# A scan kernel in which GpSimd adds two states before TensorE sums them, in 16 of 128 steps

## The chip, the cores and the metric

The kernel runs on one core of one Trainium2 chip. The metric is the time of one execution on the device in microseconds, given as the median of several runs. The profile is of one execution of its own; its times are counted from the start of its span.

The engines are named as in the profile: PE is TensorE (matmuls), PEld its weight loads, DVE is VectorE, ACT is ScalarE, POOL is GpSimd, SP is the engine that issues most transfers.

## The reference, cut to what matters

The program is two layers, each an attention-like part and an MLP, with layer norms and residuals around them. The first part is a selective scan over 512 time steps for 2 sequences, 1024 channels and 16 states per channel:

```python
def step(state, inp):
    dt_t, B_t, C_t, u_t = inp
    dA = jnp.exp(dt_t[..., None] * A)
    state = state * dA + (dt_t * u_t)[..., None] * B_t[:, None, :]
    y = jnp.einsum('bdn,bn->bd', state, C_t)
    return (state, y)
...
y = ys.transpose(1, 0, 2) + x * D
y = y * jax.nn.silu(gate)
return y @ W_out.T
```

Then follow an MLP whose weights are stored as 4-bit numbers and dequantised by the kernel, an attention over heads with single-head keys and values, and an MLP with a shared and a routed part. All sums are in fp32. The output y of a channel is a sum over its 16 states; in which order they are added is free up to rounding.

## The kernel before, in words

**The scan.** Channels lie on the 128 partitions, time along the free axis. A *block* is one sequence's chunk of 128 channels; there are 16 blocks, the eight of sequence 0 first (`order`, L993). Each block is worked in eight *steps* (`gi`) of two states (`NG = 2`), so that there are 128 steps `s`. A tile `bx` of 128 x 2 x 512 goes through four engines in a step:

- `times_B` (L1012, VectorE): bx = du x B, where du = dt x u lies in PSUM;
- `scan` (L1020, VectorE): the recurrence along time over the two states, with the decays `da`, which `exps` (L997, ScalarE) has written to PSUM;
- `times_C` (L1026, GpSimd): bx = bx x C;
- `sums` (L1030, TensorE): two matmuls with the identity add the two halves of bx to the block's sum `py` in PSUM. The first step of a block begins the sum with a matmul by diag(D).

`fin` (L1044, VectorE) multiplies the gate g by the finished sum, two steps into the next block. There is one bank for py: the next block's first matmul (L1036) waits for fin. There are six buffers for bx, so `times_B` of a step waits for the sums of six steps before.

**The order.** A loop over s writes the order of every engine's queue by hand; `pin` (L401) ties each instruction to the one before it on its engine. In the pass for step s, TensorE gets the sums of step s - 2 and some matmuls of other work; VectorE gets the product for s + 1 and the scan of s; GpSimd gets the product with C of s. An engine works through its queue strictly in this order.

**The other work of TensorE.** The generator `stream` (L956) hands out the matmuls that are to run beside the scan, one call at a time, in a fixed order. While sequence 1 is scanned these are: sequence 0's output projection (`out_tiles`, L904, `po`, L916), the transposes of the normed rows (`turned`, L777), and sequence 0's first MLP (`ffn0`, L938: for each of eleven tiles of the hidden layer four matmuls for `fg` and four for `fu`, L947). How many calls are handed out in a pass is set by a budget `free`: it grows by `STEP = 3.5` us a pass, each call costs `MM = 0.86`, the sums of the pass cost 0.86 for each matmul, and of what is unspent at most 0.86 is kept. A call can also be refused because neither of two PSUM banks is free, or because its input isn't due yet; then the budget of the pass is lost.

What is done with a result is a *job*, started two ticks (one pass) after its last matmul: for an MLP tile, ScalarE evicts the gate (L682 to L684), GpSimd multiplies (L687), and VectorE multiplies with `fu` (L935); for a row tile of the output projection, `out_job` (L865) copies it (L868), norms it (L119 to L134, L150), adds it to x (L855) and norms again. GpSimd jobs take turns (`pool_turn`).

**After the scan.** What is left of `stream` runs off. Then come sequence 1's output projection (L1124), the down projection of sequence 0's MLP (L1146), and the rest of the program. The down projection's weights are dequantised in this stage by `once` (L309): VectorE takes the nibbles out (L233) and subtracts the zeros (L322), GpSimd multiplies with the scales (L323), SP writes them to HBM (L330 for the first part, L340 for the second), from where SP loads them as `wd` (L1141). The tiles for it take the memory that the scan's tiles held. Weight tiles (w4: W_out, gate and up weights, `wd`) share three buffers.

Of the kernel before, what the change touches and what calls it, by code (L numbers as in the profile page):

```python
# [28 lines left out]
NCH = D_IN // P  # L29
N_ST = 16  # L30
# [4 lines left out]
NG = 2  # L35
NGI = N_ST // NG
# [20 lines left out]
def tile_sandwich(  # L57
# [5 lines left out]
    nc = tc.nc  # L63
# [24 lines left out]
    ident = const.tile([P, P], F32, name="ident")  # L88
# [312 lines left out]
    def pin():  # L401

        seen = nc.cur_bb.bb.instructions
        for ins in seen[behind.get("n", 0) :]:
            if ins.engine not in ORDERED:
                continue
            prev = behind.get(ins.engine)
            if prev is not None:
                tc.add_manual_dep(
                    ins, prev.name,  # L410
                    mybir.DependencyInfo(mybir.DependencyClass.NoSync, mybir.DependencyReason.DATA),
                    reason="order of tracing",
                )
            behind[ins.engine] = ins
        behind["n"] = len(seen)
# [6 lines left out]
    with ExitStack() as mamba:  # L422
# [35 lines left out]
        st = {}  # L458
# [21 lines left out]
        def diag(k):  # L480

            c = k % NCH
            t_ = dgp.tile([P, P], F32, tag="dg", name=f"dg{k}")
            nc.scalar.activation(t_, ident, AF.Copy, scale=ch[:, c, KCONV + 1 : KCONV + 2])
            st["diag", k] = t_
# [49 lines left out]
        def states(b, gi):  # L535

            for lst, lo, nm in ((Bbs[b], 0, "B"), (Cbs[b], R_C - R_B, "C")):
                t_ = bcp.tile([P, NG, S], F32, tag=f"{nm}{gi}", name=f"{nm}{b}_{gi}")
                n0 = lo + gi * NG
                ins = nc.sync.dma_start(  # L540
                    out=t_, in_=scr[b][n0 : n0 + NG, :].partition_broadcast(P)
                )
                lst[gi] = t_
            return ins

        def dt_in(b, c):
            ps = mbank(f"pv{b}_{c}")
            nc.tensor.matmul(ps, wdt[:, ts(c, P)], dtT[b], start=True, stop=True)
            return ps
# [9 lines left out]
        with ExitStack() as p1:  # L559
# [78 lines left out]
            for gi in range(NGI):  # L638
                last = states(0, gi)
# [10 lines left out]
        with ExitStack() as p2:  # L650
# [17 lines left out]
            def spawn(gen, lag=0):  # L668
                jobs.append([now[0] + lag, gen])

            def tick():
                now[0] += 1
                for job in list(jobs):
                    if job[0] <= now[0]:
                        try:
                            job[0] = now[0] + next(job[1])
                        except StopIteration:
                            jobs.remove(job)
# [13 lines left out]
            def bank_free():  # L692
                return len(turns) < 2 or turns[-2][1] is not None
# [10 lines left out]
            MM = 0.86  # L704
# [288 lines left out]
            order = [(b, c) for b in range(B) for c in range(NCH)]  # L993
            NS = len(order) * NGI
            bxs = {}

            def exps(s):  # L997
                k, gi = divmod(s, NGI)
                b, c = order[k]
                for i in range(NG):  # L1000
                    n = gi * NG + i
                    nc.scalar.activation(  # L1002
                        das[s % 2][:, i, 1:], st["dt", b, c][:, 1:], AF.Exp, scale=A[:, c, n : n + 1]
                    )

            def new_du(k):

                b, c = order[k]
                du = st["du"] = ps_du.tile([P, S], F32, tag="du", name=f"du{b}_{c}")
                nc.scalar.copy(du, st["dt", b, c])  # L1010

            def times_B(s):  # L1012
                k, gi = divmod(s, NGI)
                b, c = order[k]
                if gi == 0:
                    nc.vector.tensor_mul(st["du"], u[b][c], st["du"])
                bx = bxs[s] = bxp.tile([P, NG, S], F32, tag="bx", name=f"bx{b}_{c}_{gi}")
                nc.vector.tensor_mul(bx, st["du"].unsqueeze(1).to_broadcast([P, NG, S]), Bbs[b][gi])  # L1018

            def scan(s):  # L1020
                flat = bxs[s].rearrange("p n t -> p (n t)")
                nc.vector.tensor_tensor_scan(  # L1022
                    flat, das[s % 2].rearrange("p n t -> p (n t)"), flat, 0.0, ALU.mult, ALU.add
                )

            def times_C(s):  # L1026
                b, c = order[s // NGI]
                nc.gpsimd.tensor_mul(bxs[s], bxs[s], Cbs[b][s % NGI])  # L1028

            def sums(s):  # L1030
                k, gi = divmod(s, NGI)
                b, c = order[k]
                cost = NG * MM
                if gi == 0:
                    y = st["y"] = ps_y.tile([P, S], F32, tag="y", name=f"py{b}_{c}")
                    nc.tensor.matmul(y, st["diag", k], u[b][c], start=True, stop=False)  # L1036
                    cost += MM
                bx = bxs.pop(s)
                for i in range(NG):
                    n = gi * NG + i  # L1040
                    nc.tensor.matmul(st["y"], ident, bx[:, i, :], start=False, stop=(n == N_ST - 1))  # L1041
                return cost

            def fin(k):  # L1044

                b, c = order[k]
                nc.vector.tensor_mul(g[b][c], g[b][c], st["y"])
                st[f"fin{k}"] = now[0]

            def dt_job(k, ps):  # L1050
                dt_out(*order[k], ps)
                release(f"pv{k}")
                yield 1
# [9 lines left out]
            for s in range(NS + 3):  # L1063
                k, gi = divmod(s, NGI)
                free = min(free, MM) + STEP
                if gi == 1 and k + 1 < len(order):
                    dt_due = k + 1
                if gi == 2 and k:
                    fin(k - 1)
                for part in ((1, 0) if gi == 2 else (0, 1)):  # L1070
                    if part == 0:
                        if 0 <= s - 2 < NS:
                            free -= sums(s - 2)
                    else:
                        while free > 0 and s < NS:
                            if dt_due and bank_free():
                                turns.append([f"pv{dt_due}", None])
                                spawn(dt_job(dt_due, dt_in(*order[dt_due])), 2)
                                free -= MM
                                dt_due = None  # L1080
                            cost = next(pe, None)
                            if cost is None:
                                break
                            free -= cost
                tick()
                if gi == 4 and k + 1 < len(order):
                    diag(k + 1)
                if 0 < s < NS - 1:
                    times_B(s + 1)
                    if gi == NGI - 2 and k + 1 < len(order):  # L1090
                        new_du(k + 1)
                tick()
                if s < NS:
                    scan(s)
                    if s == 0:
                        times_B(1)
                    if s + 2 < NS:
                        exps(s + 2)
                    times_C(s)
                    if order[k] == (0, NCH - 1):  # L1100
                        states(1, gi)
                pin()
# [6 lines left out]
        with ExitStack() as p3:  # L1109
# [9 lines left out]
            for j in range(NCH // 2):  # L1119
                w = wo_pair(1, 0, j)  # L1120
                for e in range(2):
                    c = 2 * j + e
                    for i in range(TB):
                        nc.tensor.matmul(  # L1124
                            po[i], g[1][c][:, ts(i, P)], w[:, e, :],
                            start=(c == 0), stop=(c == NCH - 1),
# [9 lines left out]
            for i, m in enumerate(IC):  # L1136
                j, e = divmod(i, 2)
                if not e:
                    w = wst.tile([P, 2, H], F32, tag="w4", name=f"wd0_{j}")
                    n = len(IC[i : i + 2])  # L1140
# [4 lines left out]
                for t in range(TB):  # L1145
                    nc.tensor.matmul(  # L1146
                        fo[t], its[i][:m, ts(t, P)], w[:m, e],
                        start=(i == 0), stop=(i == len(IC) - 1),
# [279 lines left out]
```

## Time and profile before

| | |
|---|---|
| median of 3 runs | 965.91 us (965.67 to 966.76) |
| profiled execution | 963.47 us, span 961.7 us |
| mean granted TensorE clock | 0.971 |
| busy over the span | PE 90%, DVE 70%, POOL 48%, ACT 44% |
| first and last scan instruction | start at 74.2 and 568.9 us |
| products with C (L1028) | 128, 2360 ns each |
| scans (L1022) | 128, 2277 ns each |
| sums (L1041) | 512 matmul records, two to a matmul call of 128 x 512 fp32 |

Of a group's line in the profile, the first part tells line, engine and operation, what is written and read and its shape, and how often; behind the bar stand the total busy time in us and the mean of one in ns; behind the second bar the idle time of that engine just ahead of these instructions, with what ended most of it. In a timeline, a line has the start and the length in us, then the instructions that follow each other directly, merged. In a list of waits, a line has who waited for whom, the total in us, how many times, and the longest.

### The profile page before, as it was taken

How to read it: one execution, taken by the hardware profiler on the slowest of the kernel's cores; microseconds unless marked ns; L12 is line 12 of the kernel's file. 1: busy time of each engine (PE TensorE's matmuls, PEld its weight loads, DVE VectorE, ACT ScalarE, POOL GpSimd, SP SyncE). 2: the span in 40 equal slices, each digit the busy share in tenths (PEclk: the TensorE clock that was granted, in tenths of full speed). 3: DMA queues.
4: the chain of work that ended last, by engine and by line, in shares of the span. 5: the costliest groups of instructions: out<-in, count | busy, mean ns of one | idle time of the engine just before them, and what ended most of it. 6: DMA issues, size and time to landing. Idle time of an engine off the chain costs nothing.

```text
span 961.7 us, 7188 instructions
## 1 busy us (share of the span) xinstructions
PE 869.3 (90%) x2216; PEld 391.1 (41%) x2216; DVE 676.8 (70%) x783; ACT 420.7 (44%) x631; POOL 464.0 (48%) x335
## 2 busy tenths in 40 slices
PE   6967979878999799769999999998999998999994
PEld 3533433323543344324443434444544444445441
DVE  5959999999999989999989977334510024525225
ACT  4245775656667646565656421124320013412122
POOL 6656796776877757777767664330000000001002
PEclk9988999999999999999999999999999999999998
DMA  6349011100003833300110114336122231100101
GB/s 200 143 159 394 22 37 37 37 29 30 22 26 134 295 128 131 110 0 5 40 44 22 29 40 147 133 127 212 55 62 74 63 100 44 65 12 22 55 0 44
DMA packets 43816, 80.08 MB, mean 83 GB/s; under 512 B 7774, under 2 KB 20937, under 8 KB 43778
## 3 DMA queue, kind: packets, MB, share of 16 engines
q1 hardware_dynamic: 41506, 73.64, 22.6%
q0 software_dynamic: 1984, 5.47, 1.5%
q10 hardware_dynamic: 288, 0.52, 0.1%
q8 instruction: 17, 0.28, 0.1%
q14 instruction: 21, 0.17, 0.1%
HBM read 68.37 MB, written 11.24 MB: 83 GB/s over the span
## 4 chain that ended last, share of the span: by engine, by line
PE 49%; DVE 27%; issue 10%; POOL 5%; DMA 3%; ACT 1%; SPq 0%; DVEq 0%; POOLq 0%; ACTq 0%
DVE bx L1022 10%; PE py L1041 8%; DVE bx L1018 8%; PE pd L1356 6%; PE pup L1293 5%; PE fo L1146 4%; PE fu L367 3%; PE fo L1209 3%; PE fg L367 3%; PE fu L947 3%; POOL bx L1028 3%; PE po L1124 3%; PE fg L947 2%; DMA B<-scr 2%; DVE u L475 2%
## 5 line engine op out<-in xcount | busy, mean ns | idle before, releaser
L1028 POOL TENSOR_TENSOR bx<-bx,C 128x1024 f32<-128x1024 f32 x128 | 302.1, 2360 | 134.3 <-DVE bx L1022 118.1
L1022 DVE TENSOR_TENSOR_SCAN bx<-da,bx 128x1024 f32<-128x1024 f32 x128 | 291.4, 2277 | 0.1
L1041 PE MATMUL py<-bx,ident 128*128 128x512 f32 x512 | 249.0, 617 | 38.3 <-POOL bx L1028 38.2
L1002 ACT ACTIVATE da<-dt,A 128x511 f32<-128x511 f32 x256 | 176.6, 691 | 163.2 <-DVE bx L1022 158.5
L1041 PEld LDWEIGHTS py<-bx,ident 128*128 128x128 f32 x512 | 96.6, 195 | 171.9 <-issue 96.9
L1018 DVE TENSOR_TENSOR bx<-du,B 128x1024 f32<-128x1024 f32 x128 | 154.0, 1204 | 9.5 <-DMA wgu_d<-w_gu 6.2
L1222 DVE TENSOR_TENSOR it<-it,fu 128x512 f32<-128x512 f32 (+1 forms) x11 | 7.6, 687 | 73.9 <-PE fu L367 73.9
L1293 PE MATMUL pup<-hT_l,wup 128*128 128x512 f32 x128 | 57.2, 602 | 0.0
L709 PE MATMUL pg<-xT,w_g 128*128 128x512 f32 x120 | 56.3, 597 | 0.0
L1356 PE MATMUL pd<-wdn,hid 128*128 128x512 f32 x128 | 56.3, 601 | 0.0
L381 POOL TENSOR_TENSOR sd<-ve,half 128x4 f16<-128x4 f16 x2 | 2.1, 1044 | 110.5 <-DVE ve L379 110.5
L127 POOL TENSOR_TENSOR rs_lo<-ve_lo,mhalf 128x1 f32<-128x1 f32 x8 | 5.5, 683 | 78.3 <-DVE ve_lo L125 78.3
L947 PE MATMUL fu<-hT_f,wu 128*128 128x512 f32 (+1 forms) x88 | 41.5, 593 | 0.7 <-ACT dt L553 0.7
L947 PE MATMUL fg<-hT_f,wg 128*128 128x512 f32 (+1 forms) x88 | 41.6, 595 | 0.0
L367 PE MATMUL fg<-hT_f,wg 128*128 128x512 f32 (+1 forms) x88 | 40.2, 593 | 0.7 <-ACT hT_f L171 0.7
L367 PE MATMUL fu<-hT_f,wu 128*128 128x512 f32 (+1 forms) x88 | 40.7, 603 | 0.0
L475 DVE SCALAR_TENSOR_TENSOR u<-px,ch,u 128x511 f32<-128x511 f32 (+2 forms) x48 | 35.8, 746 | 6.1 <-ACT u L468 4.9
L1209 PE MATMUL fo<-wd,it 128*128 128x512 f32 (+1 forms) x88 | 39.8, 595 | 0.0
L1146 PE MATMUL fo<-wd,it 128*128 128x512 f32 (+1 forms) x88 | 38.0, 593 | 0.0
L1356 PEld LDWEIGHTS pd<-wdn,hid 128*128 128x128 f32 x128 | 24.9, 194 | 31.8 <-issue 31.2
L1293 PEld LDWEIGHTS pup<-hT_l,wup 128*128 128x128 f32 x128 | 24.5, 195 | 28.8 <-issue 28.8
L1221 ACT ACTIVATE it<-fg 128x512 f32<-128x512 f32 (+1 forms) x11 | 6.6, 597 | 65.7 <-PE fg L367 65.7
(223 smaller groups left out, 1137.8 us busy)
## 6 DMA issues: line engine op xcount, KB each, us to landing
wo<-in_W_outT SPq DMA_DIRECT2D x20, 512.0 KB
B<-scr SPq DMA_DIRECT2D x16, 512.0 KB
C<-scr SPq DMA_DIRECT2D x16, 512.0 KB
wg<-wgu_d SPq DMA_DIRECT2D x10, 512.0 KB
wu<-wgu_d SPq DMA_DIRECT2D x10, 512.0 KB
w_x<-in_W_in SPq DMA_DIRECT2D x8, 512.0 KB
wgu_d<-w_gu POOLq DMA_DIRECT2D x16, 256.0 KB, 2.3
w_g<-in_W_in SPq DMA_DIRECT2D x8, 512.0 KB
```

The lines of the kernel that those rows point to most:

```text
L367: nc.tensor.matmul(ps[:m], w[:, kc, e * P : e * P + m], hT[:, kc, :], start=(kc == 0), stop=(kc == KH - 1),)
L709: nc.tensor.matmul(ps, w[:, k, ts(e, P)], xT[b][:, k, :], start=(k == 0), stop=(k == KH - 1))
L947: nc.tensor.matmul(ps[:m], wt[j][a][:, kc, e * P : e * P + m], hT[:, kc, :], start=(kc == 0), stop=(kc == KH - 1),)
L1002: nc.scalar.activation(das[s % 2][:, i, 1:], st["dt", b, c][:, 1:], AF.Exp, scale=A[:, c, n : n + 1])
L1018: nc.vector.tensor_mul(bx, st["du"].unsqueeze(1).to_broadcast([P, NG, S]), Bbs[b][gi])
L1022: nc.vector.tensor_tensor_scan(flat, das[s % 2].rearrange("p n t -> p (n t)"), flat, 0.0, ALU.mult, ALU.add)
L1028: nc.gpsimd.tensor_mul(bxs[s], bxs[s], Cbs[b][s % NGI])
L1041: nc.tensor.matmul(st["y"], ident, bx[:, i, :], start=False, stop=(n == N_ST - 1))
L1146: nc.tensor.matmul(fo[t], its[i][:m, ts(t, P)], w[:m, e], start=(i == 0), stop=(i == len(IC) - 1),)
L1209: nc.tensor.matmul(fo[t], its[i][:m, ts(t, P)], w[:m], start=(i == 0), stop=(i == len(IC) - 1),)
L1293: nc.tensor.matmul(ps, w[:, kc, ts(e, P)], src[kc], start=(kc == 0), stop=(kc == KH - 1))
L1356: nc.tensor.matmul(pd, hid[kc][:, ts(i, P)], wdn[kc], start=(kc == 0), stop=(kc == INT // P - 1),)
```

## The change

In some steps GpSimd, after its product with C, adds the second state's half of bx to the first's, and TensorE then adds one half to py and not two. These are steps of sequence 1 alone: in its first two blocks the steps 1, 3, 5 and 7, in the next two none, in the last four the steps 1 and 5. That is 8 + 8 = 16 of 128 steps. The cost that `sums` reports to the budget falls with the number of its matmuls. In a pass whose sums are of such a step, the other matmuls are handed out ahead of the sums and not behind them, as was done before only in the pass gi = 2.

```diff
             def times_C(s):
                 b, c = order[s // NGI]
                 nc.gpsimd.tensor_mul(bxs[s], bxs[s], Cbs[b][s % NGI])
+                if paired(s):
+                    nc.gpsimd.tensor_add(bxs[s][:, 0, :], bxs[s][:, 0, :], bxs[s][:, 1, :])
+
+            def paired(s):
+
+                k, gi = divmod(s, NGI)
+
+                return order[k][0] == 1 and (k - NCH not in (2, 3) and gi in (1, 5) or k - NCH < 2 and gi % 2 == 1)
 
             def sums(s):
                 k, gi = divmod(s, NGI)
                 b, c = order[k]
-                cost = NG * MM
+                ns = 1 if paired(s) else NG
+                cost = ns * MM
...
                 bx = bxs.pop(s)
-                for i in range(NG):
-                    n = gi * NG + i
-                    nc.tensor.matmul(st["y"], ident, bx[:, i, :], start=False, stop=(n == N_ST - 1))
+                for i in range(ns):
+                    last = gi == NGI - 1 and i == ns - 1
+                    nc.tensor.matmul(st["y"], ident, bx[:, i, :], start=False, stop=last)
                 return cost
...
-                for part in ((1, 0) if gi == 2 else (0, 1)):
+                for part in ((1, 0) if gi == 2 or 2 <= s < NS + 2 and paired(s - 2) else (0, 1)):
                     if part == 0:
                         if 0 <= s - 2 < NS:
                             free -= sums(s - 2)
```

## The prediction

> **What bounds the kernel now.** I read the page's groups first, to find the scan and its per-step price:
>
> ```profile
> L1028 POOL TENSOR_TENSOR bx<-bx,C 128x1024 f32<-128x1024 f32 x128 | 302.1, 2360 | 134.3 <-DVE bx L1022 118.1
> L1022 DVE TENSOR_TENSOR_SCAN bx<-da,bx 128x1024 f32<-128x1024 f32 x128 | 291.4, 2277 | 0.1
> L1041 PE MATMUL py<-bx,ident 128*128 128x512 f32 x512 | 249.0, 617 | 38.3 <-POOL bx L1028 38.2
> ...
> L1018 DVE TENSOR_TENSOR bx<-du,B 128x1024 f32<-128x1024 f32 x128 | 154.0, 1204 | 9.5 <-DMA wgu_d<-w_gu 6.2
> ```
>
> 128 steps; in the order of time a step without extras takes 3.31 us on VectorE (scan plus product), 2.36 us on GpSimd, and four matmul records on TensorE (a call is two records). Then the busy table by stage: sequence 1's scan, the rest of the first MLP's matmuls, sequence 1's output projection, the down projection (columns: stretch, length, then busy time and records of each engine).
>
> ```profile
> 331.00:571.15 240.15, 218.53 (x498) 91.90 (x498) 229.94 (x173) 136.32 (x198) 168.98 (x91) 0.99 0.19 61
> 571.15:592.13 20.98, 20.77 (x49) 8.57 (x48) 10.06 (x21) 4.80 (x9) 8.95 (x7) 1.00 0.30 97
> 592.13:619.43 27.30, 27.30 (x65) 11.82 (x64) 14.11 (x22) 1.76 (x3) 12.67 (x12) 1.00 0.43 151
> 619.43:657.30 37.87, 37.87 (x90) 16.77 (x90) 13.16 (x40) 9.13 (x11) 11.66 (x18) 1.00 0.40 129
> ```
>
> VectorE bounds the scan (230 of 240 us); from 571 us TensorE bounds. So a matmul saved in the scan is worth nothing there; it pays only if other TensorE work moves from after the scan into it. GpSimd has 71 us free in the first row. VectorE's largest wait there:
>
> ```profile
> DVE it L935 <- PE fu L947: 5.8, 4, 2.5
> ```
>
> TensorE's order at the end of the scan:
>
> ```profile
> 573.84 1.98 PE L1041 MATMUL py<-bx,ident 128*128 128x512 f32 x4 [0.21 <-POOL bx L1028]
> 575.66 2.74 PE L947 MATMUL fu<-hT_f,wu 128*128 128x512 f32 x6
> ...
> 588.53 3.60 PE L947 MATMUL fu<-hT_f,wu 128*96 128x512 f32 x8
> 591.97 27.63 PE L1124 MATMUL po<-wo,g 128*128 128x512 f32 x64
> ```
>
> Between the last sum (575.82) and the output projection (592.13) stand 38 records, 19 calls: 16.31/19 = 0.858 us a call. Behind the projection a load is just in time:
>
> ```profile
> PEld fo L1146 <- DMA wd<-wd_d: 0.6, 1, 0.6
> ```
>
> **The Trainium skill.** "GPSIMD Engine Reference", section 3.1, gives 4497 ns for a two-input add of 2048 fp32: about 1.12 us for 512, as an estimate. The trace has the same shape:
>
> ```profile
> L687 POOL TENSOR_TENSOR it<-ti,it 128x512 f32<-128x512 f32 x8 | 10.2, 1270 | 1.0 <-ACT ti L684 1.0
> ```
>
> I use 1.27, plus 0.1 for the wait on the product before it (L134 stands 0.1 us behind L127). Section 8 says GpSimd contends with VectorE instructions with two SBUF inputs or in a two-port mode. The trace agrees: after the scan, beside GpSimd products, VectorE's two-SBUF subtraction varies,
>
> ```profile
> 589.40 0.68 DVE L322 TENSOR_TENSOR w_d<-q_d,z_d 128x512 f32<-128x512 int32 x1
> ...
> 590.46 1.65 DVE L322 TENSOR_TENSOR w_d<-q_d,z_d 128x512 f32<-128x512 int32 x1
> ```
>
> while scans (da in PSUM) stay within 2256 to 2291 ns. "TensorE: Matmul & The Clock Gate", Part 1, has half clock after idleness; the trace shows it too: at 425.31, after 3.0 us idle, four records took 3.53 us.
>
> **The change, part by part.**
>
> *Sums removed.* 16 calls x 0.858 = 13.7 us of TensorE. The planner's budget per step stays at 3.5 us, so it packs other matmuls in. The changed kernel's order shows where they came from: behind the last sum stand 6 calls instead of 19. So 13 x 0.858 = 11.2 us leave the stage that TensorE bounds. The other three are lost in the gap after sequence 0's output projection, where the planner has no matmul to give until the norms are done.
>
> *Adds.* 16 x 1.37 = 21.9 us on GpSimd. A step with one takes 2.36 + 1.37 = 3.73 against 3.31, so GpSimd falls back 0.4 us and recovers in the next step (2.36). Who waits is TensorE's sum two steps later; before the paired sums now stand up to eight other calls, which cover it. Without that cover the cost would be 1.4 us of TensorE's time per add, which has over 20 us idle in the scan. At the tail there is no cover. GpSimd's queue there is product, add (step 5), product 6, gate product of MLP tile 9, product 7; before, the gate product stood last. From 565.80: +2.35+1.37 = 569.5, +2.36 = 571.9, +1.27 = 573.1, +2.36 = 575.5, against 573.8: the last sum and fin are 1.7 us later. Stream end: 575.8 + 1.7 + 6 x 0.858 = 582.7, against 592.1: **-9.4 us**.
>
> *Down projection.* Now the load of its first weights is late next: they are dequantised after the scan. SP's queue had it at
>
> ```profile
> 615.43 0.39 SPq L1141 DMA_DIRECT2D wd<-wd_d  x1
> ```
>
> behind six writes of the second part (612.65 to 615.33); it landed about 619.4. In the changed order it stands right behind seven small loads after the last write of the first part (issued by 602.9). The first part starts 0.3 us later (fin +1.7, but no 1.4 us wait for an MLP product behind it) and loses MLP tile 10's products from its queues (GpSimd 1.7 us, and a VectorE nibble op of 2.48 instead of 0.43): about -2. So 602.9 + 0.3 - 2 + 7 x 0.65 = 605.7, landing 4 us later at 609.7. TensorE arrives at 582.7 + 27.3 = 610.0. It fits, with nothing to spare: -9.4 stays. What follows (657 us on) hangs on the down projection's end and moves whole.
>
> *Moved work that I cost at nothing.* The planner's jobs follow the matmuls: the norms of sequence 0's four tiles (VectorE statistics, GpSimd powers, ScalarE scalings) and the MLP tiles' evictions come up to three steps earlier, none more often. Their cover is that they stand in the same queues in equal number; uncovered, one bn_stats group costs VectorE 1.0 us, which is in the next item. The loads of W_out go faster through SP: in the first block a call group of five needs three 512 KB loads, of which each is issued at least 5 us before its use if a buffer is freed as the order says; the first load took 5.4 us (330.66 to 336.1) behind other loads. If a later one takes longer, TensorE waits the difference, about 1 us at most by these two numbers. The gap in which TensorE has only sums falls partly into the second block, where paired steps leave it still less to do; half clock there would lengthen a sum from 0.86 to 1.7 us a call, in steps that have 1.5 us free. The product's six buffers (bx) give the sums three steps of slack; the one wait on them (1.1 us at 345.99) lies ahead of the first pair and stays.
>
> *VectorE's scan.* fin of the first block (L1047, at 366.09) waits for TensorE. From 343.16 TensorE runs without idling; 26 calls stood up to its last sum (365.5), now 29 (368.1), since matmuls are drawn ahead. VectorE arrives about 1.0 later too (one bn_stats group is pulled ahead of it): wait about +1.1. In exchange, the 5.8 us of waits for fu: three of the four had the MLP product (L935) in the very step that issues its matmuls; now one has (tile 2), the others have one to three steps between. That leaves about 1.3: -4.4. Net -3.3; TensorE may lag in blocks 6 and 7 (35 calls in block 6 = 30.0 us against VectorE's 28.7), so I take half: **-1.5**. Bounds: +1.1 (waits stay) to -4.4 (no wait at fin).
>
> Sum on the profiled execution (963.47; span 961.7 and 1.8 around it): -9.4 - 1.5 = -10.9, giving 952.6. The median of the runs is 2.4 above that execution, so 965.9 - 10.9 = **955.0**.
>
> **Rivals.**
> - *Scan no earlier* (fin +1.1, fu waits stay): -9.4 + 1.1 = -8.3: 957.6. For it: TensorE's lag; against: the steps between. Chance 0.2.
> - *Everything lands*: -11.2 - 3.3, tail delay hidden: 951.4. Against it: the down projection's load. 0.1.
> - *The dequantised weights hold the down projection*: they follow the scan, whose end hardly moves. If the load lands at 617 instead of 610, -2.4 - 1.5 = -3.9: 962.0; for it: the load had no slack. 0.12.
> - *Slower, by shared reads*: the add reads two SBUF operands; if VectorE stood still while it runs, the scan would stretch by 16 x 1.37 = 21.9 us, net +11: 977. It decides from 10.9/16 = 0.68 us per add. Against: scans beside L687 keep 2.28. 0.08.
>
> **How the numbers follow.** The likeliest is 955.0 with 0.5; its own range 952.5 to 957. The 8-in-10 range, 950.5 to 962.5, takes in the first three rivals and leaves out the slower one. Faster than 0.2% (1.9 us, about what can be told from no change): 0.86; within: 0.05, from the third rival's edge; slower: 0.09.
>
> **What would show it.** Right: 480 sum records, 16 adds at 1.27; scans at 2.28; the output projection about 580 to 582, the down projection at 607 to 610; VectorE's wait for fu below 2 us. Wrong: a wait of the down projection on its load over 3 us, VectorE waits on py over 2 us in the first two blocks, or scans longer than 2.3.

## The result, and the profile after

The changed kernel takes 955.86 us (median of six executions, 953.32 to 959.62), against 965.79 us for the kernel before, timed in turn with it: a ratio of 0.9898, 95% interval 0.9878 to 0.9919. In a second set of runs it took 957.06 us against 964.78, ratio 0.9918 (0.9895 to 0.9942). The predicted time was 955.0 us. The size was right; the working below shows that two of its terms were not.

The profiled execution took 955.89 us, span 954.1. Of the groups of its page, the same lines as before:

```profile
L1028 POOL TENSOR_TENSOR bx<-bx,C 128x1024 f32<-128x1024 f32 x128 | 302.0, 2360 | 115.3 <-DVE bx L1022 90.7
L1022 DVE TENSOR_TENSOR_SCAN bx<-da,bx 128x1024 f32<-128x1024 f32 x128 | 291.6, 2279 | 0.1
L1050 PE MATMUL py<-bx,ident 128*128 128x512 f32 x480 | 238.1, 626 | 35.6 <-POOL bx L1028 32.3
```

There are 480 sum records in place of 512, and the scans (2279 ns) and products with C (2360 ns) are as long as before. The adds, in the groups with shapes kept apart, have the length that was taken from the MLP product of the same shape:

```profile
L1030 POOL TENSOR_TENSOR bx<-bx 128x512 f32<-128x512 f32 x16 | 20.3, 1268 | 1.3
```

Next the busy table by stage, cut at the events of this execution: sequence 1's scan, the rest up to the output projection, the output projection, the down projection.

```profile
330.12:572.69 242.57, 221.06 (x491) 92.06 (x492) 232.56 (x175) 139.78 (x205) 191.12 (x109) 0.95 0.20 64
572.69:583.89 11.20, 10.41 (x25) 3.97 (x24) 3.19 (x13) 1.59 (x3) 5.44 (x4) 1.00 0.44 131
583.89:611.52 27.63, 27.63 (x65) 11.97 (x63) 15.11 (x20) 1.76 (x3) 11.27 (x9) 1.00 0.38 131
613.15:651.19 38.04, 38.04 (x90) 16.94 (x91) 15.21 (x48) 8.94 (x11) 14.67 (x22) 1.00 0.44 135
```

The second row is where the gain lies: from the end of the scan to the first matmul of the output projection 11.20 us, where it was 20.82 before (591.97 less the scan's end at 571.15). The scan itself, 242.57 us from its first instruction at 330.12, is not shorter than before (242.41 us, 328.74 to 571.15). VectorE's waits in it changed places but not their sum, about 9 us in both. Before, beside the 5.8 us for fu that the prediction shows:

```profile
DVE bx L1018 <- issue: 1.1, 1, 1.1
DVE du L1016 <- ACT du L1010: 0.9, 1, 0.9
DVE st_mo L119 <- ACT o L868: 0.7, 1, 0.7
DVE st_f L119 <- POOL x L855: 0.4, 1, 0.4
```

After:

```profile
DVE g L1056 <- PE py L1050: 3.4, 1, 3.4
DVE bx L1018 <- issue: 1.9, 1, 1.9
DVE st_f L119 <- POOL x L855: 1.9, 2, 1.5
DVE it L935 <- PE fu L947: 1.8, 2, 1.3
```

The waits for fu fell from 5.8 to 1.8 us, and a wait of 3.4 us at a fin (L1056) is new. TensorE's order at the scan's end:

```profile
576.92 1.98 PE L1050 MATMUL py<-bx,ident 128*128 128x512 f32 x4 [0.79 <-POOL bx L1028]
578.74 1.88 PE L947 MATMUL fg<-hT_f,wg 128*96 128x512 f32 x4
580.46 3.60 PE L947 MATMUL fu<-hT_f,wu 128*96 128x512 f32 x8
583.89 27.63 PE L1133 MATMUL po<-wo,g 128*128 128x512 f32 x64
613.15 9.28 PE L1155 MATMUL fo<-wd,it 128*128 128x512 f32 x21 [1.63 <-DMA wd<-wd_d]
```

Twelve records, six calls, stand behind the last sum, and the down projection (L1155) waits 1.63 us for its first weights.

A measure that leaves out what the change doesn't touch is the time from the first scan of sequence 1 to the end of the down projection. Before it is 242.41 (scan) + 20.82 (to the output projection) + 27.46 (to the down projection) + 38.02 = 328.71 us; after it is 242.57 + 11.20 + 29.26 + 38.04 = 321.07 us. That is 7.6 us less, and 8.4 us less in the repeated run (320.33). The rest of the difference between the medians lies ahead of this stretch or behind it, where both kernels do the same; the last section comes back to it. The table gives all runs in this measure. "Calls" are those behind the last sum; "wd" is the longest time for which TensorE stood idle in the down projection until weights landed.

| kernel | median us | ratio (95%) | calls | scan | to output proj. | wd | scan to end of down proj. |
|---|---|---|---|---|---|---|---|
| before | 965.79 | | 19 | 242.4 | 20.8 | 0 | 328.7 |
| changed | 955.86 | 0.9898 (0.9878 to 0.9919) | 6 | 242.6 | 11.2 | 1.6 | 321.1 |
| changed, again | 957.06 | 0.9918 (0.9895 to 0.9942) | 6 | 241.8 | 11.2 | 1.7 | 320.3 |
| old budget | 956.55 | 0.9910 (0.9897 to 0.9924) | 15 | 237.1 | 18.9 | 0 | 321.5 |
| adds only | 970.81 | 1.0057 (1.0044 to 1.0069) | 19 | 247.6 | 21.7 | 0 | 334.7 |
| no adds | 955.13 | 0.9895 (0.9882 to 0.9909) | 6 | 241.4 | 10.9 | 1.7 | 319.6 |
| first sum at gi = 1 | 953.06 | 0.9866 (0.9848 to 0.9884) | 6 | 238.4 | 11.2 | 2.4 | 317.7 |
| old order | 951.02 | 0.9867 (0.9841 to 0.9893) | 7 | 238.1 | 12.1 | 1.9 | 317.7 |
| loads on ScalarE's queue | 959.62 | 0.9950 (0.9937 to 0.9964) | 6 | 241.7 | 11.2 | 3.7 | 323.8 |
| jobs last | 953.06 | 0.9886 (0.9860 to 0.9912) | 6 | 241.7 | 10.2 | 1.6 | 319.1 |
| last four blocks | 957.02 | 0.9920 (0.9895 to 0.9946) | 10 | 239.4 | 13.2 | 2.9 | 321.2 |
| first two blocks | 962.49 | 0.9977 (0.9960 to 0.9994) | 14 | 245.4 | 16.4 | 0 | 327.2 |
| old order, jobs last | 952.26 | 0.9873 (0.9860 to 0.9887) | 7 | 239.7 | 11.4 | 1.7 | 318.4 |
| the same, wd first | 951.49 | 0.9857 (0.9835 to 0.9879) | 7 | 239.9 | 11.4 | 0.3 | 317.5 |

The medians are each from kernels timed in turn with the kernel before, whose own median was 964.78 to 965.79 us in these sets; the ratio is the fairer comparison between rows. The stage times are from one profiled execution each. The changed kernel's two executions differ by 0.7 us in the last column, so differences of that size between rows show nothing.

### The profile page after: what moved, and what is told of

Its sections match the earlier page's. It is cut to its first block, busy times and chain, and to the rows that moved or that the text cites. A ratio compares the mean times of both kernels' runs of the same rounds, so it can differ in the third digit from the quotient of the medians.

```text
span 954.1 us, 7148 instructions
## 1 busy us (share of the span) xinstructions
PE 862.3 (90%) x2184; PEld 386.6 (41%) x2184; DVE 675.2 (71%) x783; ACT 420.2 (44%) x631; POOL 484.0 (51%) x351
## 4 chain that ended last, share of the span: by engine, by line
PE 46%; DVE 28%; issue 11%; POOL 5%; DMA 2%; ACT 1%; SPq 0%; DVEq 0%; POOLq 0%; ACTq 0%
DVE bx L1022 11%; DVE bx L1018 8%; PE pd L1365 6%; PE py L1050 5%; PE pup L1302 5%; PE fo L1155 4%; PE fu L367 3%; PE fo L1218 3%; POOL bx L1028 3%; PE fg L367 3%; PE fu L947 3%; PE fg L947 3%; PE po L1133 3%; PE po L916 2%; DVE u L475 2%
## 5 line engine op out<-in xcount | busy, mean ns | idle before, releaser
L1028 POOL TENSOR_TENSOR bx<-bx,C 128x1024 f32<-128x1024 f32 x128 | 302.0, 2360 | 115.3 <-DVE bx L1022 90.7
L1022 DVE TENSOR_TENSOR_SCAN bx<-da,bx 128x1024 f32<-128x1024 f32 x128 | 291.6, 2279 | 0.1
L1050 PE MATMUL py<-bx,ident 128*128 128x512 f32 x480 | 238.1, 626 | 35.6 <-POOL bx L1028 32.3
L1050 PEld LDWEIGHTS py<-bx,ident 128*128 128x128 f32 x480 | 91.5, 198 | 164.1 <-issue 93.1
L1155 PE MATMUL fo<-wd,it 128*128 128x512 f32 (+1 forms) x88 | 38.0, 593 | 1.6 <-DMA wd<-wd_d 1.6
L1365 PEld LDWEIGHTS pd<-wdn,hid 128*128 128x128 f32 x128 | 24.2, 190 | 30.7 <-issue 30.1
```

Source lines behind the costliest of these rows:

```text
L1022: nc.vector.tensor_tensor_scan(flat, das[s % 2].rearrange("p n t -> p (n t)"), flat, 0.0, ALU.mult, ALU.add)
L1155: nc.tensor.matmul(fo[t], its[i][:m, ts(t, P)], w[:m, e], start=(i == 0), stop=(i == len(IC) - 1),)
L1365: nc.tensor.matmul(pd, hid[kc][:, ts(i, P)], wdn[kc], start=(kc == 0), stop=(kc == INT // P - 1),)
```

## The experiments

### Is the gain the number of calls?

```diff
                 ns = 1 if paired(s) else NG
-                cost = ns * MM
+                cost = NG * MM
```

> The adds and the order of the parts are those of the changed kernel; only the budget is told that a step's sums cost two calls, as before. TensorE then has the time that the adds save but is given no other work for it, and 15 calls stay behind the last sum of the scan (before 19, changed kernel 6). Theory (the gain is the number of calls that leave the stretch behind the scan, 0.858 us each): 4 calls x 0.858 = 3.4 us of gain, less a later last sum of about 1.4 us: about 964, which is 2 us below before. Rival (fewer matmuls of the sum shorten the scan or the tail by themselves): as the changed kernel, about 956.

The time was 956.55 us, as that of the changed kernel, with 15 calls behind the last sum. The theory of the gain fell. VectorE's waits in this kernel's scan:

```profile
DVE it L935 <- PE fu L947: 2.3, 1, 2.3
DVE bx L1018 <- POOL bx L1030: 1.2, 1, 1.2
DVE st_f L119 <- POOL x L855: 0.4, 1, 0.4
```

These are 3.9 us in place of 9, and the scan is 237.1 us in place of 242.6. TensorE was given nothing for the time it saved, so it fell behind VectorE less often, and the new wait at fin is missing. Against the changed kernel: 9 calls more behind the scan, +7.7 us; the scan -5.4; no wait for wd and a start of the down projection straight behind the output projection, -1.8; together +0.4, within the scatter (321.45 against 321.07). A saved sum can thus be cashed in two ways, as a call taken out of the stretch behind the scan, or as a shorter wait of VectorE in it. For these nine calls, what the changed kernel gained by the first it lost almost wholly by the second and at the load. The rival's time came true, and one half of its reason: the scan is 5.3 us shorter than before the change. The other half did not: at the tail the saved matmuls shorten nothing by themselves, for there only the four missing calls count (18.9 against 20.8 us, with 1.5 us lost to a later last sum).

### What do the adds cost?

In the first run both halves are still added by TensorE (the second state is counted twice in those steps); in the second the adds are left out (and with them the second state of those steps).

```diff
-                ns = 1 if paired(s) else NG
+                ns = NG
...
-                for part in ((1, 0) if gi == 2 or 2 <= s < NS + 2 and paired(s - 2) else (0, 1)):
+                for part in ((1, 0) if gi == 2 else (0, 1)):
```

> The adds are made, but TensorE still adds both halves in every step, in the old order (so the second state is counted twice in those 16 steps). The cost of the adds alone. Theory: they lie in GpSimd's free time, only the last sum of the scan comes later: 0 to +2 us against before, 966 to 968. Rival (each add holds VectorE or TensorE up, and the change pays this from a larger gain): up to 16 x 1.37 = +22 us, with scans longer than 2.28 us or a scan stage longer than 240 us.

```diff
-                if paired(s):
-                    nc.gpsimd.tensor_add(bxs[s][:, 0, :], bxs[s][:, 0, :], bxs[s][:, 1, :])
```

> The changed kernel without its adds: the second half of those 16 steps is left out of y. The same 6 calls stay behind the last sum. Theory: what the adds cost in the changed kernel is the later last sum only, so about 1.5 us less than the changed kernel, 954.4, or the same time if the first load of the down projection's weights, for which the changed kernel waits 1.6 us, holds the start. Rival (the adds cost more, in the scan too): 3 to 5 us less than the changed kernel, with a shorter scan stage.

The adds alone cost 5.5 us (970.81 against 965.29), neither 0 to 2 nor 22. In the list of TensorE's waits between 328 and 585 us, and in VectorE's within the scan, this kernel has

```profile
PE py L1050 <- POOL bx L1030: 7.6, 7, 2.6
```

```profile
DVE it L935 <- PE fu L947: 9.6, 5, 2.8
```

TensorE, which is as full as before, waits for the adds; what it then issues later, fu, VectorE waits for: 9.6 us in place of 5.8. So the adds are not free where TensorE's saving doesn't pay for them. With the saving they nearly are: without them the changed kernel takes 955.13 us, 0.7 less, with intervals that overlap. In the measure of the table they cost 0.8 to 1.5 us, hardly more than its scatter: 0.4 to 1.2 in the scan and 0.3 at the last fin.

### Where does the new wait at fin come from?

TensorE's order around the last sum of sequence 1's first block, in the changed kernel:

```profile
365.10 1.02 PE L916 MATMUL po<-wo,g 128*128 128x512 f32 x2
366.05 1.12 PE L548 MATMUL pv<-dtT,wdt 33*128 33x512 f32 x2
367.10 2.84 PE L916 MATMUL po<-wo,g 128*128 128x512 f32 x6
369.78 1.02 PE L1050 MATMUL py<-bx,ident 128*128 128x512 f32 x2
```

Five calls stand ahead of that sum, drawn in by the new order of the parts in pass gi = 1. VectorE needs the sum in the next pass.

```diff
-                for part in ((1, 0) if gi == 2 or 2 <= s < NS + 2 and paired(s - 2) else (0, 1)):
+                for part in ((1, 0) if gi == 2 or 2 <= s < NS + 2 and gi != 1 and paired(s - 2) else (0, 1)):
```

> The changed kernel, except that in the passes gi = 1 the sums stand ahead of the other matmuls even where the step is a paired one. The last sums of a block, which fin waits for, are then not behind calls that the saved matmul let in. Six calls behind the last sum, as in the changed kernel. Theory A (the wait of 3.4 us at the first fin comes from the calls drawn ahead of the sum): the wait falls below 1.5 us, the scan ends 2 to 3 us earlier, time about 953. Theory B (the wait comes from TensorE's late start in that block and the half clock there, or another wait takes its place): no difference from the changed kernel, 956.

The sum is then issued at 366.01, and the wait at fin is gone from the list of VectorE's waits in the scan:

```profile
DVE st_f L119 <- POOL x L855: 1.9, 2, 1.5
DVE it L935 <- PE fu L947: 1.8, 2, 1.3
DVE bx L1018 <- POOL bx L1030: 1.1, 1, 1.1
```

The scan is 238.4 us, 3.4 to 4.1 less than in the two runs of the changed kernel, and the time 953.06 us. Theory A holds. Theory B falls for another reason too: in the changed kernel's second execution the mean granted clock in the first block was 0.94 in place of 0.83, and the wait was 3.42 us again. It is not the adds either: without them it was 3.42 us as well. Then the whole order of the parts was put back to that of before:

```diff
-                for part in ((1, 0) if gi == 2 or 2 <= s < NS + 2 and paired(s - 2) else (0, 1)):
+                for part in ((1, 0) if gi == 2 else (0, 1)):
```

> The changed kernel, but in the passes with a paired step's sums TensorE gets the sums first and the other matmuls behind them, as before the change (7 calls behind the last sum). Theory (an add is late for TensorE unless other calls stand ahead of its sum; the waits then push VectorE's waits for fu back up, as with the adds alone, where the scan of sequence 1 became 5 us longer): scan stage 2 to 5 us longer than the changed kernel's 242.6, time 958 to 961. Rival (TensorE has so much time in the scan that the order is worth nothing): 956, as the changed kernel; or better, 952, since the wait at the first fin goes as in the run with the sums first at gi = 1.

951.02 us; ratio to before 0.9867, and in the table's measure 317.7 us, the same as with gi = 1 alone. The theory's direction was wrong, and the rival's second figure right. TensorE does wait for the adds now,

```profile
PE py L1050 <- POOL bx L1030: 9.5, 4, 4.3
```

but VectorE's waits for fu stay at 1.8 us: the saved matmuls give TensorE the time for it. (In a later kernel with the same order in the scan, "old order, jobs last", they were 3.3 us, still well below the 9.6 of the adds alone.) What the reordering buys is one call behind the scan, 0.9 us, and its cost, the wait at fin, is larger.

### Each half of the change alone

First the pairs of the last four blocks alone, then those of the first two.

```diff
-                return order[k][0] == 1 and (k - NCH not in (2, 3) and gi in (1, 5) or k - NCH < 2 and gi % 2 == 1)
+                return order[k][0] == 1 and k - NCH > 3 and gi in (1, 5)
```

> Pairs in the last four blocks alone, eight of the sixteen; 10 calls stay behind the last sum, 9 have left. Theory (each saved sum is either a call less behind the scan or a shorter wait of VectorE within it; the four waits for fu lie in blocks 13 to 15, the added wait at fin in block 9): the waits for fu fall as in the changed kernel and fin of block 8 is not waited for, scan stage about 238; 9 x 0.858 = 7.7 and 4 us of scan, less 1.5 at the tail: about 955 to 957. Rival (gain in proportion to the adds): half of the changed kernel's, 961.

```diff
-                return order[k][0] == 1 and (k - NCH not in (2, 3) and gi in (1, 5) or k - NCH < 2 and gi % 2 == 1)
+                return order[k][0] == 1 and k - NCH < 2 and gi % 2 == 1
```

> Pairs in the first two blocks of sequence 1 alone, the other eight of the sixteen; 14 calls stay behind the last sum, 5 have left. Theory (the order of the changed kernel costs the wait of 3.4 us at the first fin, and the waits for fu of the last blocks lie too far off to be helped fully): 5 x 0.858 = 4.3 us of calls less, scan stage 241 to 244 against 242.4, nothing at the tail: 960 to 962. Rival (the two halves of the change add up: the changed kernel's 9.9 less the 8.1 of the last four blocks): 963 to 964, or (each saved sum is worth the same) half of 9.9: 961.

The last four blocks alone give 957.02 us, with half of the adds most of the gain: the scan is 3.0 us shorter than before, 9 calls have left (20.8 to 13.2 us), and 2.9 us are lost in the middle of the down projection to a load. The first two blocks alone give 962.49 us, 2.3 us of gain: five calls leave (20.8 to 16.4), but the scan is 3.0 us longer, with the wait of 3.42 us at the first fin and 5.2 us for fu. The scan stage lay above the 241 to 244 that was expected. Gains of the halves sum to 10.4 us and the whole gives 7.7 to 9.9; that fits the rival's reason, that the halves add up, within what these medians can tell, though its figure of 963 to 964 was a little high.

### The tail and the load

In this run the jobs of the last pass stand behind the last product with C:

```diff
-                tick()
+                if s != NS - 1:
+                    tick()
...
-                tick()
+                if s != NS - 1:
+                    tick()
                 if s < NS:
                     scan(s)
...
+                if s == NS - 1:
+                    tick()
+                    tick()
```

> The changed kernel, but in the last pass the two ticks, which start the MLP jobs, come behind the last product with C and not ahead of it, so that tile 9's gate product no longer stands ahead of the last product with C in GpSimd's queue. Theory (the last sum is late by that gate product of 1.27 us, not by the adds: without the adds it was late by nearly as much): from the scan's end to the last fin 5.0 us in place of 6.2. What it brings: 1.2 us less than the changed kernel, 954.7, if the dequantising, which follows that fin, comes forward with it, and nothing if the load of wd holds the down projection. Rival (the add of step 5 delays it): 6.2 stays, and so does the time.

GpSimd's timeline then has the last two products directly behind the add, and the gate product behind them:

```profile
568.62 1.27 POOL L1030 TENSOR_TENSOR bx<-bx 128x512 f32<-128x512 f32 x1
569.84 4.65 POOL L1028 TENSOR_TENSOR bx<-bx,C 128x1024 f32<-128x1024 f32 x2
574.45 1.27 POOL L687 TENSOR_TENSOR it<-ti,it 128x512 f32<-128x512 f32 x1
```

From the scan's end to the last fin it is 5.20 us in place of 6.25 (before 4.71; without the adds 5.92). So of the later last sum, 1.05 us are the gate product's and about 0.3 the add's. The median is 953.06 us; the interval (0.9860 to 0.9912) overlaps those of the changed kernel, so the times alone do not show the gain. The wait for wd is as it was (1.58 us), since the dequantising came forward as much as the last sum: from the scan's end to the load of its zeros (z_d) it is 10.8 us in place of 11.8.

Now the load of wd. SP's timeline in the changed kernel has

```profile
603.75 0.36 SPq L330 DMA_DIRECT2D wd_d<-w_d  x1
604.16 2.99 SPq L227 DMA_DIRECT2D s_d<-in_down_s  x4
607.20 2.17 SPq L227 DMA_DIRECT2D z_d<-zd_d  x3
609.48 0.96 SPq L1150 DMA_DIRECT2D wd<-wd_d  x2
```

The issue of the first part's last write ends at 604.1, and wd is issued 5.4 us later, behind seven small loads. The next run takes these small loads out of SP's queue.

```diff
-        def words(parts, n, name):
+        def words(parts, n, name, eng=nc.sync):
...
-            word_loads(parts, 0, n, qw, z, s, 1, nc.sync, nc.sync)
+            word_loads(parts, 0, n, qw, z, s, 1, eng, eng)
...
-        for j, w in words(parts, hw, "d1"):
+        for j, w in words(parts, hw, "d1", nc.scalar):
```

> The changed kernel, but the small loads of the second dequantised part are issued from ScalarE's queue, so that the first load of wd stands in SP's queue directly behind the last write of the first part. Theory (the wait of 1.6 us is SP's order: the load is issued only at 609.5, behind z_d loads that wait): the load is issued by 605, the wait goes, time 1.6 us less than the changed kernel, 954.3. Rival (the load follows the writes, or the transfers are slow together): the wait stays, 956.

The first load is issued at 605.31 and not waited for, but the down projection stops halfway instead, for a load of the second part:

```profile
610.93 20.76 PE L1155 MATMUL fo<-wd,it 128*128 128x512 f32 x48
635.39 19.03 PE L1155 MATMUL fo<-wd,it 128*128 128x512 f32 x40 [3.70 <-DMA wd<-wd_d]
```

The time is 959.62 us, and in the table's measure 2.8 us worse than the changed kernel. Both sentences of the expectation were half right: SP's order did set the first wait, and taking it away made a later one. The other way, keeping all on SP's queue and putting wd ahead of only the last three of the small loads, was tried on the best order (old order, jobs last), with that order beside it:

> The pairs of the changed kernel with the sums first as before the change, and in the last pass the jobs behind the last product with C. Theory (the gain of the old order, 4.8 us, and of the later jobs, up to 2.8 us, are of two places): scan stage 238, scan's end to the last fin 5.0, together 1 to 2.5 us less than the old order alone: 948.5 to 950. Rival (the down projection waits on its load either way, which follows SP's order, not the last fin): 951, as with the old order alone, and a wait of 3 us on wd.

```diff
...
+            for _ in range(PACK):
+                next(dqg)
+            wds = {0: load_wd(0)}
             for _ in dqg:
                 pass
...
+                    w = wds[j] if j in wds else load_wd(j)
```

> As the one before, and the first load of the down projection's weights stands in SP's queue three small loads further ahead, between those of the scales and of the zeros of the second part. Theory (that queue order sets the wait of about 2 us): wd is issued 2 us earlier, the wait falls below 0.5 us and the down projection starts 2 us earlier: 947 to 948. Rival (the second part, dequantised that much later, then holds the down projection, as with the loads on ScalarE's queue): a wait of 2 to 4 us in the middle of the down projection, no gain, 949 to 951.

With the jobs last, but wd where it was, the time is 952.26 us: not better than the old order alone (951.02, on another chip; its scan was 1.6 us shorter in the profiled execution), and the wait for wd was 1.7 us, not the rival's 3. With wd three loads ahead, SP's timeline is

```profile
596.61 3.00 SPq L227 DMA_DIRECT2D s_d<-in_down_s  x4
599.78 0.38 SPq L1151 DMA_DIRECT2D wd<-wd_d  x1
600.20 2.20 SPq L227 DMA_DIRECT2D z_d<-zd_d  x3
```

The load is issued 34.8 us after the scan's end and not 37.1, the down projection starts straight behind the output projection (27.47 us after it, as before the change), and 0.25 us is waited in its middle. In the table's measure that is 0.9 us. The median is 951.49 us, ratio 0.9857; the difference to 952.26 is not resolved. The changed kernel ran on that chip as well (957.06, 0.9895 to 0.9942), and the interval of this version (0.9835 to 0.9879) lies clear of it, as does that of the version before it (0.9860 to 0.9887). Of the three edits, the runs show what the old order brings; what the other two add to it is too small for these times to tell.

Last, the changed kernel once more, for that comparison:

> The changed kernel once more, beside the following kernels on one chip. 955 to 957 by its first runs, ratio to before 0.988 to 0.992.

It took 957.06 us, a ratio of 0.9918: at the upper ends of both ranges.

## Why the prediction was right, and where it was not

**Sums removed.** Right. There are 480 records and six calls behind the last sum, and the stretch to the output projection is shorter by 9.62 us: 11.2 of calls less a last sum that is 1.54 us later (6.25 against 4.71 us behind the scan's end). The term said -9.4, with 1.7 for the delay. Its cause was named as the add and the gate product's new place; the gate product has most of it.

**Adds.** Right in size: 1268 ns each against 1.27 taken from the trace. The estimate of 1.12 us for 512 elements, in proportion to the figure for 2048 in the Trainium skill's "GPSIMD Engine Reference", section 3.1, was low by 0.14 us. The rival of shared reads fell: scans beside the adds took 2279 ns on average.

**Their cover.** The prediction costed the adds at nothing because other calls now stand ahead of the paired sums, and put 1.4 us of TensorE's time per add on the order without that. The old order shows that the cover was not needed; its other reason, that TensorE has over 20 us idle in the scan, was the better half of that step. The adds without the saving show when a cover would be: there each cost 5.5/16 = 0.34 us.

**VectorE's scan: the step that failed.** It was put at -1.5, as half of -4.4 (fu) + 1.1 (fin); that half is -1.65, a slip too small to matter. The first figure was good: 5.8 to 1.8, -4.0. The second was 3.42, in both executions. The count of calls up to the last sum (29) was right. VectorE's arrival was not: one statistics group was added to its way (about 0.8 us), but two waits in the same block (0.7 for the copied row, 0.9 for du in the trace before) went, and they were not taken off. From the product that waits for bx to fin, VectorE needed 20.1 us before and 19.2 after, where about 21.1 was predicted; TensorE, up to the end of the last sum, needed 19.5 and 22.5, with 22.1 predicted. Smaller waits, 0.8 more on bx (0.1 in the second execution) and 1.5 more for a normed row of x, took the rest, and the scan's length hardly changed: +0.2 and, in the second execution, -0.6 in place of -1.5. What stood ahead of the sum, and so the wait, came from the new order of the parts, as the two runs that put that sum first again show. The outcome was that of the rival "scan no earlier", worked out there as 957.6, but not by its reason: the waits for fu did not stay, the wait at fin took their place.

**Down projection.** "It fits, with nothing to spare" was off by 1.6 us. TensorE was ready at 611.5, but wd was issued at 609.5, where 605.7 was predicted. Of the 3.8 us, 1.4 are the later start of the scan in this execution, and wd was issued 5.4 us behind the last write and not 4.6, because of the seven loads. The first part's last write came 1.5 us later still than worked out. The 2 us for the MLP products that left its queues did come: from the first subtraction to the end of that write's issue it was 17.7 us before and is 15.8 now. What did not come are the 1.4 us of the wait for an MLP product behind fin. That wait is gone, but the first subtraction waits for the zeros z_d, and their load stands in SP's queue behind a load of weights, which waits for TensorE (SP's wait there ends with the matmuls of fg before and of fu now) until a buffer is free. Before, it stood behind one of wu:

```profile
575.86 0.69 DVE L1047 TENSOR_TENSOR g<-g,py 128x512 f32<-128x512 f32 x1 [4.73 <-PE py L1041]
581.86 0.38 SPq L111 DMA_DIRECT2D wu<-wgu_d  x1
582.29 0.61 SPq L227 DMA_DIRECT2D z_d<-zd_d  x1
585.22 0.69 DVE L322 TENSOR_TENSOR w_d<-q_d,z_d 128x512 f32<-128x512 int32 x1 [4.73 <-DMA z_d<-zd_d]
```

Now it stands behind one of W_out:

```profile
578.94 0.69 DVE L1056 TENSOR_TENSOR g<-g,py 128x512 f32<-128x512 f32 x1 [3.66 <-PE py L1050]
584.09 0.39 SPq L862 DMA_DIRECT2D wo<-in_W_outT  x1
584.51 0.61 SPq L227 DMA_DIRECT2D z_d<-zd_d  x1
588.33 1.29 DVE L322 TENSOR_TENSOR w_d<-q_d,z_d 128x512 f32<-128x512 int32 x2 [3.48 <-DMA z_d<-zd_d]
```

From fin to the first subtraction it is 9.4 us in both. No run here moves that load, so what moving it would bring is not shown.

**The sum.** For the stretch of the table -9.4, -1.5 and 0 were predicted, together -10.9; it gave -9.6, +0.2 and +1.8, which is -7.6. From the same start of 965.9 that would be 958.3 us, outside the prediction's own range of 952.5 to 957. The medians differ by 9.9 in one set of runs and by 7.7 in the other. So the closeness of 955.0 is in part luck, from differences outside the stretch, and what happened in the stretch was, in size, the prediction's first rival plus a wait of 1.6 us for a load.

**Its signs.** The records, the adds, the scans and the wait for fu came as listed. The output projection began at 583.9, not at 580 to 582, and the down projection at 613.2, not at 607 to 610; 1.4 us of each is the later start of the scan. One of the signs of being wrong came as well: VectorE waited on py for 3.4 us in the first block, where 2 was the limit. The other two did not: the wait for wd was 1.6 us, with 3 as the limit, and the scans stayed at 2.28.

**What the prediction didn't see.** It treated the calls as the gain and the waits as an extra, and held that a matmul saved in the scan is worth nothing there. The old budget contradicts that: with nine of the thirteen calls left where they were, the scan is 5.3 us shorter than before, and the time is that of the changed kernel. Nor do the two exclude each other, except in the changed kernel's order: with the old order twelve calls leave and the scan is still 4.3 us shorter than before.

## What to carry to other kernels

Work saved on an engine that follows the bottleneck can be spent on moving other work forward, or left as slack that shortens the bottleneck's waits for it; more work forward is only better if nothing that the bottleneck waits for stands behind it in the queue. So after such a change, list the bottleneck's waits again, and look at what stands ahead of the instruction that each of them names. When an order is turned to cover a wait, test the old order with the rest of the change in place, since the saving itself may already be the cover.

## What the runs showed of the hardware

The same instructions behind the down projection took between 299.6 and 306.2 us, whichever the kernel. Two executions in the busy table, from the end of the down projection to the end of the program, the first of the old order and the second of the kernel with the sum first at gi = 1:

```profile
648.57:948.20 299.63, 279.15 (x792) 132.30 (x790) 107.58 (x245) 73.45 (x113) 22.24 (x40) 0.97 0.19 62
```

```profile
648.68:954.80 306.12, 285.72 (x792) 136.16 (x790) 107.49 (x245) 73.34 (x113) 22.19 (x40) 0.95 0.19 61
```

The same 792 matmul records were busy 6.6 us longer at a mean granted clock of 0.95 in place of 0.97. The start of sequence 1's scan, ahead of which the kernels are the same, lay between 325.2 and 331.0 us. Differences of a few us between single executions say nothing on the change; the stage that it touches does.

In the scan's third block, where TensorE has little but sums, the mean granted clock was 0.84 in the changed kernel and 1.00 before, and the block's length hardly differed (32.0 and 31.6 us). VectorE was busy for 29.9 us of it and for 30.7 before, so it stood idle 1.3 us longer, and the slower TensorE cost no more than that there.
